# Short groups of a mixture of experts: output columns in fourths of TensorE's columns, and one scatter of short rows per group

## The chip, the core and the metric

The kernel runs on one core of a Trainium2 chip. The metric is the device time of one execution in microseconds (us), as the median of several runs. A profile of one execution gives every instruction's start and length on the core's engines: TensorE (PE, with its weight loads shown apart as PEld), VectorE (DVE), ScalarE (ACT), GpSimd (POOL) and SyncE (SP).

## What is computed

A block of a Perceiver: a cross attention from 8 x 64 tokens to 1601 context rows, a causal linear attention with an MLP, and a mixture of eight experts, all in fp32. The change lies in the mixture of experts:

```python
def _L0_ffn_ref(hidden_states, w_router, w0, w1, wo):
    ...
    x = hidden_states.reshape(-1, h)             # 512 tokens of 512 values
    router_logits = x @ w_router
    top_w, top_i = jax.lax.top_k(router_logits, K)          # K = 2 of 8 experts
    top_w = jax.nn.softmax(top_w.astype(jnp.float32), axis=-1).astype(x.dtype)
    gating = jnp.zeros((t, e), dtype=x.dtype).at[jnp.arange(t)[:, None], top_i].add(top_w)
    out = jnp.zeros_like(x)
    for ei in range(e):
        hmid = jax.nn.silu(x @ w0[ei]) * (x @ w1[ei])       # 1024 hidden values
        out = out + gating[:, ei:ei + 1] * (hmid @ wo[ei])
    return out.reshape(b, s, h)

...
x = x + _L0_ffn_ref(_layernorm(x, axis=-1), L0_ffn_w_router, L0_ffn_w0, L0_ffn_w1, L0_ffn_wo)
```

## The kernel before

All engines run the order in which the source writes their instructions (`tc.manual_schedule` names TensorE, VectorE, ScalarE, GpSimd and SyncE). The first 380 us are the two attentions, the MLP and the router; they are not touched, but for a few constants made at the start.

**The expert stage.** The router's result is turned into tables that list, for each expert, the tokens it has. Each expert takes its first 128 tokens as a whole tile (`whole_tile`, L1736). Its weights come by SyncE's queue into a ring of twelve 1 MB tiles: four `e_up` tiles, one for each fourth of the 1024 hidden values (`up_of`), and two `e_wo` tiles (`down_of`). A whole tile forms four up products (L1747; weights stationary, 128 tokens moving, 128 columns at a time), each followed by a SiLU on ScalarE and a product on VectorE (`gated`, L1703), and then eight products with `e_wo` (L1763) that gather in one PSUM bank. Of these eight, three are held back: `rest(0)`, `rest(1)` and `rest(2)` of the tile, which are passed on as `fill(k)` and put between steps that would leave TensorE waiting. The last of them is followed by `add_rows` (L1710): ScalarE multiplies by the gate, and GpSimd adds the rows to the output in HBM by an indirect DMA (L1726). GpSimd also fetches token rows by indirect DMA (`fetch`, L1663), for expert e + 2 while expert e runs. The scatters all write the output tensor, and each waits for the one before it.

**Tokens beyond 128.** They are taken by a branch at run time (`few_or_fill`, L2095, and `few_tokens`, L2085): none, one group of at most 32 tokens (`group`, L1800), or three groups of 32 (`three_groups`, L1844); there are copies of both bodies for every expert. With this input the experts have 133, 104, 217, 159, 87, 132, 70 and 122 tokens, so experts 0, 3 and 5 run `group` and expert 2 runs `three_groups`.

**A group.** With 32 tokens, the tokens are the stationary operand and take only 32 of TensorE's 128 columns. Four such products run beside each other, in four column fourths, each with its own moving operand; their results lie in four partition fourths of one PSUM bank. NQ is 4, R is 32, REST is 96.

- The up product (L1809 or L1864): column fourth q has the q-th fourth of the hidden values, 512 columns (both halves of the gated unit) moving.
- `gated`, and two transposes (`ht`, L1820 or L1876), whose result VectorE copies to SBUF (`hidT`, L1822 or L1878): hidden values on partitions, and for each fourth q its 32 tokens.
- The down product (`yq`, L1827 or L1884): column fourth q multiplies the hidden values of fourth q by the matching rows of `e_wo`, all 512 output columns moving. So the bank holds four partial sums, one in each partition fourth.
- Both halves of the bank are copied to SBUF (`parts`), and a product with `fold`, a 128 x 32 matrix of four stacked identities, adds the four partition fourths (L1841; in `three_groups` L1896, with all three groups in one bank).
- `add_rows` scales by the gate and scatters rows of 2 KB: 32 rows, or 96 for three groups.

In `group` the order on TensorE is: the transposes of the group's tokens and of the next expert's (`turn_next`), the up product, fill(0), the transposes of the hidden tile, fill(1), the down product, fill(2), the fold. In `three_groups` it is: up 0, up 1, turn 0, up 2, turn 1, down 0, turn 2, down 1, down 2, `turn_next`, the three fills, the folds.

PSUM has eight banks here: three of side 0, two of side 1 (`side_bank(1, ...)`, used in turn), and the single banks y0, y1 and yw (`y_bank`).

Of the kernel before, what the change touches and what calls it, by code (L numbers as in the profile page):

```python
# [15 lines left out]
F32 = mybir.dt.float32  # L16
# [4 lines left out]
P = 128  # L21
# [12 lines left out]
NQ = 4  # L34
# [9 lines left out]
NIDLE = 8  # L44
NS = 2
TWICE = 3
# [4 lines left out]
def perceiver_kernel(  # L51
# [186 lines left out]
    for i in range(NIDLE):  # L238
        n = 2 if i < TWICE else 1
        nc.tensor.matmul(  # L240
            idle_bank[:, : n * P],
            ident,
            ident[:, None, :].to_broadcast([P, n, P]),
            start=True,
            stop=True,
        )
# [1394 lines left out]
    if True:  # L1641


        def side_bank(side, name):
            return pse.tile([P, 512], F32, tag=f"mm{side}", bufs=3 - side, name=name)
# [153 lines left out]

        def group(e, up_of, down_of, fill, turn_next):  # L1800
# [21 lines left out]
            nc.vector.tensor_copy(h_t.rearrange("p j q -> p (j q)"), bank[:, : 2 * P])  # L1822
            fill(1)
            bank = side_bank(1, f"yq_{nm}")
            for j in range(2):
                for q in range(NQ):
                    nc.tensor.matmul(  # L1827
                        bank[q * R : (q + 1) * R, :],
                        h_t[:, j, q * R : (q + 1) * R],
                        down_of[q // 2][:, 2 * (q % 2) + j, :],  # L1830
                        start=(j == 0),
                        stop=(j == 1),
                    )
            parts = moe2.tile([P, D], F32, tag="parts3", bufs=3, name=f"parts_{nm}")
            halves = [slice(n * D // 2, (n + 1) * D // 2) for n in range(2)]
            nc.vector.tensor_copy(parts[:, halves[0]], bank[:, halves[0]])
            nc.scalar.copy(parts[:, halves[1]], bank[:, halves[1]])
            fill(2)
            y = y_bank(1, f"y_{nm}")
            for n in range(2):  # L1840
                nc.tensor.matmul(y[:R, halves[n]], fold, parts[:, halves[n]], start=True, stop=True)  # L1841
            add_rows((e, 1), [y], R, 1)

        def three_groups(e, up_of, down_of, fill, turn_next):  # L1844
# [12 lines left out]
            hid, h_t, sums, parts = {}, {}, {}, {}  # L1857
# [22 lines left out]
            def down(g):  # L1880
                bank = sums[g] = side_bank(1, f"yq_{nm}_{g}")
                for j in range(2):
                    for q in range(NQ):
                        nc.tensor.matmul(  # L1884
                            bank[q * R : (q + 1) * R, :],
                            h_t[g][:, j, q * R : (q + 1) * R],
                            down_of[q // 2][:, 2 * (q % 2) + j, :],
                            start=(j == 0),
                            stop=(j == 1),
                        )  # L1890
                parts[g] = moe2.tile([P, D], F32, tag="parts3", bufs=3, name=f"parts_{nm}_{g}")

            halves = [slice(n * D // 2, (n + 1) * D // 2) for n in range(2)]

            def folded(g, n):
                nc.tensor.matmul(  # L1896
                    y[g * R : (g + 1) * R, halves[n]], fold, parts[g][:, halves[n]], start=True, stop=True
                )
# [9 lines left out]
            down(1)  # L1908
            nc.vector.tensor_copy(parts[1], sums[1])
            down(2)  # L1910
            nc.vector.tensor_copy(parts[2][:, halves[0]], sums[2][:, halves[0]])
            nc.scalar.copy(parts[2][:, halves[1]], sums[2][:, halves[1]])
# [3 lines left out]

            y = y_bank(1, f"y3_{nm}")
            for g, n in [(0, 0), (1, 0), (2, 0), (0, 1), (1, 1), (2, 1)]:
                folded(g, n)
            add_rows((e, 1), [y], REST, 1)  # L1920

        if True:

            def late_places():
                nc.vector.tensor_tensor(late[:, 0, :, 0], late[:, 0, :, 0], late[:, 1, :, 0], ALU.add)
                src, dst = places(late[:, 0, :, 0], NE * NI, "late")
                for e in range(NE):
                    for i in range(2):
                        k = NI * e + i
                        slots[e, i] = (src[:, k : k + 1], dst[:, k : k + 1])  # L1930

# [188 lines left out]
            for e in range(NE):  # L2120
                turns = {}

                def between(k, e=e, turns=turns):
                    if k == 0 and e < NE - 1:
                        hint_ahead(e)
                    if e == 0 and k == 0:
                        late_places()
# [136 lines left out]
```

## Time and profile before

| | |
|---|---|
| median of 3 runs | 609.11 us (609.05 to 609.19) |
| profiled execution | 608.81 us |
| its span, first to last instruction | 607.1 us |
| mean granted TensorE clock | 0.996 |
| expert stage, from the first up product of expert 0 | 382.4 us on |
| expert 0's group, transposes to the next expert | 401.17 to 411.87 us |
| expert 2's three groups | 452.25 to 474.35 us |
| expert 3's group | 493.13 to 504.08 us |
| expert 5's group | 544.46 to 555.16 us |
| last scatter starts | 600.63 us |
| indirect scatters to the output | 11 of whole tiles and groups, 2 halves of the last tile |

Times within the profile count from the first instruction. PE busy is the time in which a matmul streams or drains; the matmuls are pipelined, so the recorded length of one (0.6 us for 512 columns) is more than the step to the next (0.43 us). "x16" in a line of the timeline is the number of passes merged into it; one fp32 product is two passes. The text in brackets says how long the engine had been idle and what ended that.

### The profile page before, as it was taken

The page shows a single profiled execution, that of the slowest core. Times are in us where ns is not written, and L with a number is a line of the kernel's source. Part 1 is how long each engine was busy: PE and PEld are TensorE (multiplying, and loading weights), DVE is VectorE, ACT ScalarE, POOL GpSimd, SP SyncE. Part 2 cuts the span into 40 slices and gives each one's busy share as a digit, 9 for nine tenths or more (in the row PEclk, how much of TensorE's full clock was granted, in tenths as well). Part 3 has the DMA queues.
Part 4 walks back from the last instruction along what each step waited for, and adds up shares of the span by engine and source line. Part 5 has one row for each costly group of instructions (what it writes and reads, how often), then busy time and mean ns, then how long its engine had stood idle before and what let it go on. Part 6 is the DMA issues. An engine that isn't in the chain of part 4 may idle for free.

```text
span 607.1 us, 9506 instructions
## 1 busy us (share of the span) xinstructions
PE 594.3 (98%) x3798; PEld 394.6 (65%) x3798; DVE 186.1 (31%) x450; ACT 152.7 (25%) x319; POOL 198.8 (33%) x266
## 2 busy tenths in 40 slices
PE   8999999999999999999999999999999999999994
PEld 6543434343477777668888758949772848775793
DVE  4121414234502667875104245411212111111100
ACT  3241314131136656333112311301001101001010
POOL 4000000000179987876996012342300121301112
PEclk9999999999999999999999999999999999999998
DMA  8999999999702003221236413259670959687411
GB/s 335 418 420 419 417 419 415 422 419 410 314 2 69 2 3 139 71 70 39 101 139 253 160 72 131 85 160 372 241 258 3 350 169 391 212 291 289 169 21 18
DMA packets 24087, 131.88 MB, mean 217 GB/s; under 512 B 4388, under 2 KB 4644, under 8 KB 12632
## 3 DMA queue, kind: packets, MB, share of 16 engines
q1 hardware_dynamic: 19496, 122.36, 50.9%
q0 software_dynamic: 3424, 7.61, 5.3%
q10 hardware_dynamic: 1104, 1.07, 0.5%
q8 instruction: 40, 0.66, 0.4%
q14 instruction: 23, 0.19, 0.1%
HBM read 126.08 MB, written 4.94 MB: 216 GB/s over the span
## 4 chain that ended last, share of the span: by engine, by line
PE 61%; DMA 23%; issue 13%; DVE 1%; ACT 1%; POOLq 1%; SPq 0%; POOL 0%; DVEq 0%
DMA out_dram<-y_sb,dst_late 15%; PE side L1163 8%; PE sc L481 7%; PE av L542 7%; DMA xg<-mn_dram,src_late 6%; PE v L627 5%; PE wk L788 4%; PE wq L788 4%; PE mlp L1249 3%; PE wo L999 3%; PE xo L576 2%; PE shared L1277 2%; PE up L1747 2%; DMA ctxT<-in_ctx_T_dram 2%; PE pw L407 2%
## 5 line engine op out<-in xcount | busy, mean ns | idle before, releaser
L1747 PEld LDWEIGHTS up<-xgT,e_up 128*128 128x128 f32 x896 | 100.7, 192 | 3.9 <-issue 2.1
L1747 PE MATMUL up<-xgT,e_up 128*128 128x128 f32 x896 | 101.6, 275 | 0.5 <-PEq L2149 0.3
L1726 POOL DMA_INDIRECT out_dram<-y_sb,dst_late x11 | 16.7, 1521 | 144.7 <-ACT y_sb L1717 108.0
L1763 PE MATMUL y<-e_wo,mid 128*128 128x512 f32 (+1 forms) x144 | 59.1, 549 | 0.0
L1707 DVE TENSOR_TENSOR mid<-up,act 128x256 f32<-128x256 f32 x38 | 16.1, 424 | 135.0 <-ACT act L1705 130.0
L590 POOL TENSOR_TENSOR h_sums<-h_t 128x256 f32<-128x256 f32 x1 | 0.7, 728 | 143.9 <-PE avt L569 143.9
L481 PE MATMUL sc<-ctxT,pw_t 128*64 128x401 f32 (+1 forms) x256 | 46.6, 503 | 0.3 <-DMA ctxT<-in_ctx_T_dram 0.3
L1705 ACT ACTIVATE act<-up 128x256 f32<-128x256 f32 x38 | 14.6, 383 | 119.5 <-PE up L1747 94.1
L542 PE MATMUL av<-ctx,eT 128*64 128x512 f32 x192 | 44.0, 595 | 0.0
L1763 PEld LDWEIGHTS y<-e_wo,mid 128*128 128x128 f32 x144 | 25.7, 190 | 23.0 <-issue 20.8
L481 PEld LDWEIGHTS sc<-ctxT,pw_t 128*64 128x64 f32 x256 | 17.7, 136 | 27.6 <-issue 26.2
L1163 PE MATMUL side<-v_sb,sum_w 128*128 128x256 f32 x128 | 30.5, 380 | 0.2 <-DVE v_sb L590 0.2
L542 PEld LDWEIGHTS av<-ctx,eT 128*64 128x64 f32 x192 | 13.7, 136 | 25.7 <-issue 24.8
L627 PE MATMUL v<-wv,h_t 128*128 128x512 f32 x64 | 29.2, 597 | 0.0
L922 DVE RECIPROCAL rden<-rden 128x512 f32<-128x512 f32 x8 | 26.8, 3344 | 1.4 <-ACT rden L915 1.4
L1163 PEld LDWEIGHTS side<-v_sb,sum_w 128*128 128x128 f32 x128 | 24.2, 190 | 3.9 <-issue 0.6
L1249 PE MATMUL mlp<-w,hid_sb 128*128 128x512 f32 (+1 forms) x50 | 22.3, 583 | 0.0
L489 ACT ACTIVATE scores<-sc,pb 128x401 f32<-128x401 f32 (+1 forms) x16 | 9.5, 591 | 46.6 <-PE sc L481 46.6
L498 DVE TENSOR_REDUCE negmax<-scores 128x1 f32<-128x1601 f32 x4 | 7.3, 1821 | 42.5 <-ACT scores L489 42.5
L627 PEld LDWEIGHTS v<-wv,h_t 128*128 128x128 f32 x64 | 11.6, 190 | 13.0 <-issue 12.5
L1666 POOL DMA_INDIRECT xg<-mn_dram,src_late x16 | 16.6, 1035 | 10.2 <-DVE dst_late L1660 5.7
L1186 ACT ACTIVATE hid_sb<-hid_sb,col 128x256 f32<-128x256 f32 (+1 forms) x16 | 9.8, 615 | 29.8 <-DVE hid_sb L1220 21.1
(372 smaller groups left out, 955.5 us busy)
## 6 DMA issues: line engine op xcount, KB each, us to landing
e_up<-in_L_ffn_up_dram SPq DMA_DIRECT2D x32, 1024.0 KB
ctx<-in_ctx_dram SPq DMA_DIRECT2D x24, 1024.0 KB
ctxT<-in_ctx_T_dram SPq DMA_DIRECT2D x24, 802.0 KB
e_wo<-in_L_ffn_wo_dram SPq DMA_DIRECT2D x16, 1024.0 KB
w<-in_L_attn_w_dram SPq DMA_DIRECT2D x8, 1024.0 KB
ctxT<-in_ctx_T_dram SPq DMA_DIRECT2D x8, 796.0 KB
wv<-in_L_attn_wv_dram SPq DMA_DIRECT2D x2, 1024.0 KB
wq<-in_L_attn_wq_dram SPq DMA_DIRECT2D x2, 1024.0 KB
```

The source lines that it names most:

```text
L481: nc.tensor.matmul(sc[h * S : (h + 1) * S, :width], pw_t[:, c, (2 * t + h) * S : (2 * t + h + 1) * S], keys[h][:, c, :], start=(c == 0), s ...
L542: nc.tensor.matmul(av[h * S : (h + 1) * S, :], e_t[:, 4 * g + j, h * S : (h + 1) * S], rows[h][:, j, :], start=(g == 0 and j == 0), stop=F ...
L627: nc.tensor.matmul(bank, h_t[:, c, t * P : (t + 1) * P], wv_n[:, c, :], start=(c == 0), stop=(c == KC - 1))
L788: nc.tensor.matmul(bank[:, :HT], weights[:, c, :], rows[:, c, :], start=(first and c == 0), stop=(c == 1), skip_group_check=True,)
L922: nc.vector.reciprocal(rden, rden)
L999: nc.tensor.matmul(wo_banks[t][:, part], row, weight, start=(start and j == js[0]), stop=(rows is None and j == nj - 1), skip_group_check= ...
L1163: nc.tensor.matmul(bank[:, :HT], weights[:, c, :], rows[:, c, :], start=(first and c == 0), stop=(c == 1), skip_group_check=True,)
L1249: nc.tensor.matmul(acc[t][:, part], hid[:, t * P : (t + 1) * P], w[:, part], start=False, stop=(f == FF // P - 1), skip_group_check=True,)
L1666: nc.gpsimd.indirect_dma_start(out=xg[:n, :], out_offset=None, in_=mn_dram, in_offset=bass.IndirectOffsetOnAxis(ap=slots[key][0][:n, :], a ...
L1726: nc.gpsimd.indirect_dma_start(out=rows, out_offset=bass.IndirectOffsetOnAxis(ap=where[:n, :], axis=0), in_=y_sb[:n, part], in_offset=None ...
L1747: nc.tensor.matmul(bank[:, m * P : (m + 1) * P], up_of[q][:, c, m * P : (m + 1) * P], xg_t[c], start=(c == 0), stop=(c == KC - 1),)
L1763: nc.tensor.matmul(bank[:, :width], h_t[:, j * P : (j + 1) * P], w[:, 2 * (q % 2) + j, n * width : (n + 1) * width], start=(q + j == 0), s ...
```

## The change

The kernel after the change splits the down product of a group the other way. Column fourth n holds output columns 128 n to 128 n + 127, and every one of the eight chunks of hidden values is multiplied in all four fourths: the same stationary tokens in each, 128 moving columns instead of 512. The bank's partition fourth n then holds the finished sums of 32 tokens for 128 output columns, and nothing has to be folded.

Gates and destinations must be spread to the four partition fourths as well. `spread_gates` does that for the gates, in each group or once for three groups, by a product with `fold`; `late_quarters` and `spread_places` do it once for all destinations, in expert 0's whole tile. The output is seen as rows of 128 values (four for each token), and each group is scattered by itself, as 128 rows of 512 bytes. In `group` VectorE scales the rows, in `three_groups` ScalarE, VectorE and ScalarE. New constants are made on GpSimd at the start, and the idle matmuls at the start are cut differently.

```diff
-NIDLE = 8
+NIDLE = 5
...
-TWICE = 3
+TWICE = 1
...
-        n = 2 if i < TWICE else 1
+        n = 3 if i < TWICE else 2
...
+    spread = const.tile([P, NQ, R], F32, name="spread")
+    for q in range(NQ):
+        nc.gpsimd.tensor_copy(spread[:, q, :], fold)
+    in_group = const.tile([P, NQ - 1], F32, name="in_group")
+    nc.gpsimd.memset(in_group, 0.0)
+    which_quarter = const.tile([P, 1], F32, name="which_quarter")
+    for q in range(NQ):
+        nc.gpsimd.memset(which_quarter[q * R : (q + 1) * R, :], float(q))
+        if q < NQ - 1:
+            nc.gpsimd.memset(in_group[q * R : (q + 1) * R, q : q + 1], 1.0)
...
+        out_quarters = out.rearrange("t (n d) -> (t n) d", n=NQ)
+        DQ = D // NQ
+
+        def in_quarters(bank, hid, moving, columns, start, stop):
+
+            for q in range(NQ):
+                nc.tensor.matmul(bank[q * R : (q + 1) * R, columns], hid(q), moving(q), start=start, stop=stop)
+
+        def spread_gates(e, groups, nm):
+
+            mine = moe2.tile([P, NQ - 1], F32, tag="gates_of", name=f"gates_of_{nm}")
+            nc.vector.tensor_scalar(mine[:REST, :], in_group[:REST, :], slots[e, 1][2][:REST, :], None, ALU.mult)
+            bank = side_bank(1, f"gates_{nm}")
+            in_quarters(
+                bank, lambda q: fold[:REST, :], lambda q: mine[:REST, :groups], slice(0, groups), True, True
+            )
+            gates = moe2.tile([P, NQ - 1], F32, tag="gates", name=f"gates_{nm}")
+            nc.vector.tensor_copy(gates[:, :groups], bank[:, :groups])
+            return gates
+
+        def down_chunks(y, g, h_t, j, down_of, first, last):
+
+            for q in range(NQ):
+                in_quarters(
+                    y,
+                    lambda n: h_t[:, q * R : (q + 1) * R],
+                    lambda n: down_of[q // 2][:, 2 * (q % 2) + j, n * DQ : (n + 1) * DQ],
+                    slice(g * DQ, (g + 1) * DQ),
+                    first and q == 0,
+                    last and q == NQ - 1,
+                )
+
+        def add_quarters(e, g, y, gates, by_vector):
+
+            y_sb = moe2.tile([P, DQ], F32, tag="ysq", bufs=3, name=f"y_sq_{e}_{g}")
+            rows, gate = y[:, :DQ], gates[:, g : g + 1]
+            if by_vector:
+                nc.vector.tensor_scalar(y_sb, rows, gate, None, ALU.mult)
+            else:
+                nc.scalar.activation(y_sb, rows, AF.Copy, scale=gate)
+            k = e * (NQ - 1) + g
+            nc.gpsimd.indirect_dma_start(
+                out=out_quarters,
+                out_offset=bass.IndirectOffsetOnAxis(ap=dst_quarters[:, k : k + 1], axis=0),
+                in_=y_sb,
...
+                compute_op=ALU.add,
+            )
+
         def group(e, up_of, down_of, fill, turn_next):
...
+            gates = spread_gates(e, 1, nm)
             fill(1)
-            bank = side_bank(1, f"yq_{nm}")
+            y = y_bank(1, f"yq_{nm}")
             for j in range(2):
-                for q in range(NQ):
-                    nc.tensor.matmul(
...
-            parts = moe2.tile([P, D], F32, tag="parts3", bufs=3, name=f"parts_{nm}")
...
+                down_chunks(y, 0, h_t[:, j, :], j, down_of, j == 0, j == 1)
             fill(2)
-            y = y_bank(1, f"y_{nm}")
-            for n in range(2):
-                nc.tensor.matmul(y[:R, halves[n]], fold, parts[:, halves[n]], start=True, stop=True)
-            add_rows((e, 1), [y], R, 1)
+            add_quarters(e, 0, y, gates, True)
...
             up(0)
             up(1)
             turn(0)
             up(2)
+            gates = spread_gates(e, NQ - 1, nm)
             turn(1)
-            down(0)
-            nc.scalar.copy(parts[0], sums[0])
-            turn(2)
...
+            for g in range(3):
+                ys[g] = (y_bank if g == 2 else side_bank)(1, f"yq_{nm}_{g}")
+                down(g)
+                add_quarters(e, g, ys[g], gates, g == 1)
+                if g == 0:
+                    turn(2)
             turn_next()
             for k in range(3):
                 fill(k)
-
-            y = y_bank(1, f"y3_{nm}")
-            for g, n in [(0, 0), (1, 0), (2, 0), (0, 1), (1, 1), (2, 1)]:
-                folded(g, n)
-            add_rows((e, 1), [y], REST, 1)
...
+            def late_quarters(dst):
...
+                nc.vector.tensor_copy(dst_f, dst.rearrange("p (e i) -> p e i", i=NI)[:, :, 1])
+                rows = moe.tile(by_group, F32, name="dst_groups")
+                nc.vector.tensor_tensor(
...
+            def spread_places(rows):
...
+                nc.tensor.matmul(
+                    bank[:, :n],
+                    spread.rearrange("p q r -> p (q r)"),
+                    rows.rearrange("p e g -> p (e g)"),
...
+                nc.vector.tensor_scalar(dst_quarters, bank[:, :n], float(NQ), which_quarter, ALU.mult, ALU.add)
...
                     if e == 0 and k == 1:
+                        spots_of["rows"] = late_quarters(spots_of["dst"])
                         few_of.extend(load_few())
+                    if e == 0 and k == 2:
+                        spread_places(spots_of["rows"])
```

More of the change, by code (lines that the diff above doesn't have):

```diff
@@ L1798, in whole_tile @@
             return rest
+        out_quarters = out.rearrange("t (n d) -> (t n) d", n=NQ)
[35 more added lines that the diff above has]
+                in_=y_sb,
+                in_offset=None,
+                bounds_check=NQ * (B * S + P) - 1,
+                oob_is_err=True,
+                compute_op=ALU.add,
+            )
         def group(e, up_of, down_of, fill, turn_next):
@@ L1822, in group @@
             nc.vector.tensor_copy(h_t.rearrange("p j q -> p (j q)"), bank[:, : 2 * P])
+            gates = spread_gates(e, 1, nm)
             fill(1)
-            bank = side_bank(1, f"yq_{nm}")
+            y = y_bank(1, f"yq_{nm}")
             for j in range(2):
-                for q in range(NQ):
[L1827 to L1833, printed above, removed]
-            parts = moe2.tile([P, D], F32, tag="parts3", bufs=3, name=f"parts_{nm}")
-            halves = [slice(n * D // 2, (n + 1) * D // 2) for n in range(2)]
-            nc.vector.tensor_copy(parts[:, halves[0]], bank[:, halves[0]])
-            nc.scalar.copy(parts[:, halves[1]], bank[:, halves[1]])
+                down_chunks(y, 0, h_t[:, j, :], j, down_of, j == 0, j == 1)
             fill(2)
-            y = y_bank(1, f"y_{nm}")
-            for n in range(2):
-                nc.tensor.matmul(y[:R, halves[n]], fold, parts[:, halves[n]], start=True, stop=True)
-            add_rows((e, 1), [y], R, 1)
+            add_quarters(e, 0, y, gates, True)
         def three_groups(e, up_of, down_of, fill, turn_next):
@@ L1855, in three_groups @@
             nc.vector.tensor_copy(xg_t3.rearrange("p c q -> p (c q)"), bank[:, : KC * REST])
-            hid, h_t, sums, parts = {}, {}, {}, {}
+            hid, h_t, ys = {}, {}, {}
             def up(g):
@@ L1880, in down @@
             def down(g):
-                bank = sums[g] = side_bank(1, f"yq_{nm}_{g}")
                 for j in range(2):
[L1883 to L1898, printed above, removed]
+                    down_chunks(ys[g], 0, h_t[g][:, j, :], j, down_of, j == 0, j == 1)
             up(0)
@@ L1903, in three_groups @@
             up(2)
+            gates = spread_gates(e, NQ - 1, nm)
             turn(1)
-            down(0)
-            nc.scalar.copy(parts[0], sums[0])
-            turn(2)
[L1908 to L1912, printed above, removed]
+            for g in range(3):
[4 more added lines that the diff above has]
+                    turn(2)
             turn_next()
@@ L1930, in late_places @@
                         slots[e, i] = (src[:, k : k + 1], dst[:, k : k + 1])
+                return dst
+            dst_quarters = moe.tile([P, NE * (NQ - 1)], mybir.dt.uint32, name="dst_quarters")
+            def late_quarters(dst):
+                by_group = [P, NE, NQ - 1]
+                dst_f = moe.tile([P, NE], F32, name="dst_f")
+                nc.vector.tensor_copy(dst_f, dst.rearrange("p (e i) -> p e i", i=NI)[:, :, 1])
+                rows = moe.tile(by_group, F32, name="dst_groups")
+                nc.vector.tensor_tensor(
+                    rows,
+                    dst_f[:, :, None].to_broadcast(by_group),
+                    in_group[:, None, :].to_broadcast(by_group),
+                    ALU.mult,
+                )
+                return rows
+            def spread_places(rows):
+                n = NE * (NQ - 1)
+                bank = side_bank(1, "dst_quarters")
+                nc.tensor.matmul(
+                    bank[:, :n],
+                    spread.rearrange("p q r -> p (q r)"),
+                    rows.rearrange("p e g -> p (e g)"),
+                    start=True,
+                    stop=True,
+                )
+                nc.vector.tensor_scalar(dst_quarters, bank[:, :n], float(NQ), which_quarter, ALU.mult, ALU.add)
+            spots_of = {}
             few = moe.tile([P, NE], F32, name="few")
@@ L2126, in between @@
                     if e == 0 and k == 0:
-                        late_places()
+                        spots_of["dst"] = late_places()
                         for key in [(0, 1), (1, 0), (0, 0), (1, 1), (2, 0), (2, 1)]:
```

## The prediction

> **What bounds the kernel now.** The page first, then the timeline of one expert with few tokens beyond its 128.
>
> ```profile
> span 607.1 us, 9506 instructions
> PE 594.3 (98%) x3798; PEld 394.6 (65%) x3798; DVE 186.1 (31%) x450; ACT 152.7 (25%) x319; POOL 198.8 (33%) x266
> ```
>
> TensorE (PE) is busy for 594.3 of 607.1 us, and its longest waits for others in the expert stage are 0.3 us each. So the time moves by what TensorE executes and by the new waits that its program order meets. The profiled execution took 608.81 us, 1.7 more than its span; the median of the runs is 609.11, 0.30 above it. My sum is a difference, put on the median. The short groups run four times: L1809 has 96 passes (32 for each of experts 0, 3 and 5, `group`), L1864 96 (expert 2, `three_groups`). One fp32 product is two passes in the trace.
>
> The timeline of expert 0's group (start, length, engine, line), lines of fast weight loads left out:
>
> ```profile
> 406.75 0.44 PE L1820 MATMUL ht<-ident,mid 128*128 128x128 f32 x2
> ...
> 407.02 1.02 PE L1763 MATMUL y<-e_wo,mid 128*128 128x512 f32 x2
> ...
> 407.22 0.42 DVE L1822 COPY hidT<-ht 128x256 f32<-128x256 f32 x1 [0.53 <-PE ht L1820]
> ...
> 407.98 1.92 PE L1827 MATMUL yq<-e_wo,hidT 128*32 128x512 f32 x16
> ...
> 409.83 1.13 PE L1763 MATMUL y<-e_wo,mid 128*128 128x512 f32 x2
> ...
> 410.89 1.05 PE L1841 MATMUL y<-parts,fold 128*32 128x256 f32 x4
> ...
> 411.87 14.56 PE L1747 MATMUL up<-xgT,e_up 128*128 128x128 f32 x128
> ```
>
> The reader should see that fill(1), the product at 407.02, hides the 0.42 us copy of the transposed tile, and that fill(2) at 409.83 hides the copies of the parts. The fold at 410.89 is the only part of the old ending that TensorE pays for. Expert 2:
>
> ```profile
> 464.03 0.44 PE L1876 MATMUL ht<-ident,mid 128*128 128x128 f32 x2
> ...
> 464.40 1.92 PE L1884 MATMUL yq<-e_wo,hidT 128*32 128x512 f32 x16
> 464.58 0.42 DVE L1707 TENSOR_TENSOR mid<-up,act 128x256 f32<-128x256 f32 x1 [3.18 <-ACT act L1705]
> ...
> 470.69 2.74 PE L1763 MATMUL y<-e_wo,mid 128*128 128x512 f32 x6
> ...
> 473.36 1.06 PE L1896 MATMUL y<-parts,fold 128*32 128x256 f32 x12
> ```
>
> Here turn(1) starts at 464.03, as soon as the third up product has streamed, while VectorE is still to form that group's hidden tile (to 465.00).
>
> **Removed: the fold.** In `group`, from fill(2) to the next expert's first product it is 411.87 - 409.83 = 2.04 us. Without the fold fill(2) takes 0.54 for its first pass (409.83 to 410.37, by the records) and 0.43 for its second (weight loads of L1763 follow each other every 0.43 us), so 0.97. Coming back from the 32-column shape costs a little more: from the first up product to the first y product it is 14.39 us after a group (411.87 to 426.26), 14.29 where none precedes (525.79 to 540.08). Gain 2.04 - 0.97 + 0.10 = **1.17 us**. In `three_groups` six passes of 0.43 from 470.69 end at 473.27, and the next expert starts at 474.35: gain 1.08 + 0.10 = **1.18**. The copies of the parts on VectorE and ScalarE go too; they lie beside fill(2) and are worth nothing.
>
> **Changed: the down product.** Before, 16 passes in 4 sets of four, 512 columns each, from 407.98 to 409.83: 4 x 0.43 + 0.13 to drain. After, 64 passes in 16 sets of 128 columns: as many streamed columns, four times the instructions. The trace has no 32-column product with 128 moving columns. From below: pure streaming, 0.43/4 = 0.107 a set, no change. From above: the weight load (109 ns, mean of L1827) not hidden at all, 0.217 a set, +1.75 a group. The nearest rows are the sets of four 64x64 products in the attention, here from the chain of waits:
>
> ```profile
> 198.94 0.46 PE nd L902 x32
> 199.40 0.47 PE qk L869 x32
> ```
>
> 32 passes, eight sets, in 0.47: 0.058 a set, where 64 columns stream in 0.054, though one load takes 135 ns. So loads hide, with some 5 ns a set over. The up product, 128 passes of 128 columns in 14.37 us, gives the same: 0.112. I take 0.112: 16 x 0.112 + 0.13 = 1.92, **+0.07 a group**; six groups, three of them in expert 2 (+0.22).
>
> The records of L902 show matmuls of one set starting 6 to 7 ns apart. [...]
>
> **Added: the gates, on the path.** `spread_gates` puts a VectorE product (`mine`), four one-column TensorE products and a copy ahead of fill(1). TensorE takes its program in order, so fill(1) stands behind the gates' product, which waits for `mine`, which stands behind the copy of the transposed tile on VectorE. Copy ends 407.22 + 0.42 = 407.64. A small VectorE operation takes about 0.16 (L1518 0.17) and may start 0.08 before its predecessor ends (423.65 against 423.31 + 0.42): `mine` runs 407.56 to 407.72. From VectorE's end to TensorE's start is 0.06 (406.27 + 0.42 to 406.75). The gates' product: the drain of 0.13 above plus 0.03 to 0.11 for its second pass, taken as 0.20. So fill(1) loads at 407.98 instead of 406.92: **+1.06 a group**. Fill(1) then hides nothing, since the copy is long done; the down product is what is late next, by the same 1.06. In expert 2 the gates stand between the third up product and turn(1), and `mine` behind the hidden tile that ends at 465.00: 465.08, + 0.06 + 0.20 = 465.34 against 464.03, **+1.31**. The bounds: 0.20 (the product alone, if nothing held it) and 1.5 (each VectorE step as dear as a copy from PSUM, 0.42, and each hop doubled).
>
> **Added once.** `spread_places` is two passes behind expert 0's y products: four passes of the router took 0.44 (378.30 to 378.74), so **+0.22**. Its input, two VectorE operations, is ready near 398.4, the product comes at 401.1; gone late it would cost its lateness. The idle matmuls at the start have the same 1,408 columns in 10 passes instead of 16; they end at 5.99, and the next product waits for VectorE until 6.87: 0, with 0.9 us of cover. GpSimd's twelve new setup steps (about 1.5 us by rows of 0.10 and 0.18) delay a memset that nobody waits for.
>
> **Moved: the scatters.** A group's rows go as 128 rows of 512 bytes, for 32 of 2 KB: the same bytes. Expert 2 has four scatters for two, and each waits for the landing of the one before:
>
> ```profile
> 474.43 1.59 POOL L1726 DMA_INDIRECT out_dram<-y_sb,dst_late  x1 [35.38 <-ACT y_sb L1717]
> 485.60 1.46 POOL L1726 DMA_INDIRECT out_dram<-y_sb,dst_late  x1 [9.58 <-DMA out_dram<-y_sb,dst_late]
> 487.36 1.09 POOL L1666 DMA_INDIRECT xg<-mn_dram,src_late  x1 [0.30 <-issue]
> ```
>
> Behind them on GpSimd's queue are the fetches of expert 5, at 487.36 now. At worst four scatters of 11 us from 468.3 hold them until 512; landed after 4 us (the median) they are there at 516, and TensorE turns that tile at 522.77. The cover is 6 us; a fetch as slow as the slowest (11.4) would cost under 1 us. No later wait on the output tiles follows, since these have two and three buffers, and GpSimd is idle before the last scatters (16.50 us). SP's weight loads are released by TensorE and shift with it. I take 0.
>
> **The sum.** Groups: 3 x (1.06 + 0.07 - 1.17) = -0.1. Expert 2: 1.31 + 0.22 - 1.18 = +0.35. Expert 0: +0.22. Together **+0.45 us: 609.6 us**. The change removes four folds and pays for them with four waits.
>
> **The rivals.** *A, faster: the gates cost no wait.* If the gates' product finds its input ready, each place pays 0.20 instead of 1.06 or 1.31: groups 3 x -0.90, expert 2 -0.76, expert 0 +0.22, together -3.2: **605.9**. For it speaks that `mine` needs nothing of the group; against it, the trace has all engines in written order. *B, slower: code.* The short groups' code is longer, and jumps pass over it. TensorE's branches, from the views of the two lines (count, then least, median and greatest ns):
>
> ```profile
> L2096 PEldq COMPARE_BRANCH  x6: 77/92/4305, 396.1 to 539.2; - x6
> L2090 PEldq COMPARE_BRANCH  x8: 80/248/4747, 396.2 to 554.2; - x8
> ```
>
> Two took 4.3 and 4.7 us, and work queued ahead hid them: the 4.7 us from 539.4 ended 0.3 before the transposes at 544.46. At the end of expert 2's group the branch comes 3.06 us ahead of the next product (471.29 to 474.35) and took 0.19; as slow as the two, it would cost 4.3 to 4.7 less 3.1, about 1.4, and one more such jump nearly hidden 0.3: +0.45 + 1.7, **611.3**. It decides from the point where a jump lasts longer than the queued work. [...] *C, much slower: loads not hidden.* 6 x 1.75 less the 0.44 counted: +10.5, **619.6**; the 64x64 rows speak against it.
>
> **How the numbers follow.** Forecast 0.48, A 0.21, B 0.23, C 0.08. A measurement here can tell about 0.2% (1.2 us) from no change, so the forecast, whose own range is 608.5 to 610.4, falls within it; A is faster; B and C, with some mishaps of the forecast, are slower: 0.21, 0.48, 0.31. The range reaches half into A and beyond B: 606.0 to 612.3.
>
> **What would show it.** Fill(1) some 1.0 us later after the transposes, led by a wait for VectorE's `mine`; a down product of 1.9 us; no fold, with the next up product 0.97 after fill(2); four scatters in expert 2. Fill(1) straight after the transposes speaks for A, a TensorE gap at a branch for B, sets of 0.2 us for C. I am wrong if TensorE's order isn't the written one, or a set of four isn't 0.112.

## The result and the profile after

| | before | after |
|---|---|---|
| median | 609.08 us (608.87 to 609.24, 6 runs) | 613.74 us (612.62 to 615.48, 6 runs) |
| profiled execution | 608.81 us | 613.95 us |
| mean granted clock of the runs | 0.996 in the profiled one | 0.991 to 0.996 |

The changed kernel is slower by 0.8%, clear of the spread of the runs: ratio 1.0077, interval 1.0067 to 1.0087. The page of the changed kernel:

```profile
span 612.2 us, 10138 instructions
PE 593.4 (97%) x4090; PEld 403.4 (66%) x4090; DVE 187.3 (31%) x460; ACT 148.8 (24%) x312; POOL 204.2 (33%) x280
```

TensorE is busy for 0.9 us less than before, and the span is 5.1 us longer: it stands idle for longer (and a stretch at half clock, shown below, counts as busy). The timeline of expert 0's group:

```profile
407.55 0.44 PE L1881 MATMUL ht<-ident,mid 128*128 128x128 f32 x2
408.02 0.42 DVE L1883 COPY hidT<-ht 128x256 f32<-128x256 f32 x1 [0.53 <-PE ht L1881]
408.36 0.22 DVE L1821 TENSOR_SCALAR gates_of<-in_group,xg 96x3 f32<-96x3 f32 x1
...
408.73 0.24 PE L1816 MATMUL gates<-gates_of,fold 96*32 96x1 f32 x8 [0.74 <-DVE gates_of L1821]
...
408.90 1.12 PE L1773 MATMUL y<-e_wo,mid 128*128 128x512 f32 x2
...
409.96 1.96 PE L1816 MATMUL yq<-e_wo,hidT 128*32 128x128 f32 x64
...
411.84 1.12 PE L1773 MATMUL y<-e_wo,mid 128*128 128x512 f32 x2
...
412.80 0.38 PE L1757 MATMUL up<-xgT,e_up 128*128 128x128 f32 x2
```

It shows what was forecast: fill(1) waits for `mine` (named `gates_of`), the down product takes 1.88 us (409.96 to 411.84) and no fold follows. The next expert's product, the last line, starts 0.96 us after fill(2). The end of expert 2's three groups, and TensorE's waits in the expert stage (line waited at, releaser: us, times, longest):

```profile
466.30 0.44 PE L1924 MATMUL ht<-ident,mid 128*128 128x128 f32 x2
...
472.55 0.66 PE L1705 MATMUL xgt<-ident,xg 128*128 128x128 f32 x4
...
473.04 2.74 PE L1773 MATMUL y<-e_wo,mid 128*128 128x512 f32 x6
...
478.03 2.29 PE L1757 MATMUL up<-xgT,e_up 128*128 128x128 f32 x10 [2.25 <-issue]
```

```profile
PE gates L1816 <- DVE gates_of L1821: 3.4, 4, 1.2
PE up L1757 <- issue: 2.3, 1, 2.3
```

Between the fills and expert 3's first product TensorE stands for 2.25 us with nothing to wait for that the profile shows. The view of the branch line, with its greatest value, says what its sequencer did (count, least, median and greatest ns):

```profile
L2148 PEldq COMPARE_BRANCH  x8: 80/376/5842, 399.1 to 558.7; - x8
```

The 5.84 us belong to the jump at the end of expert 2's three groups, over its one-group body and the path without few tokens. It begins at 472.02 and ends at 477.86. Before, it took 0.19 us, as the view of the same line there shows for 470.5 to 473 us:

```profile
L2090 PEldq COMPARE_BRANCH  x1: 192/192/192, 471.2 to 471.2; - x1
```

Then the granted clock, in windows over the same place (length, busy PE, clock, DMA share, GB/s):

```profile
478.00:478.50 0.50, 0.47 (x3) 0.73 1.01 426
478.50:481.50 3.00, 3.00 (x16) 0.50 1.02 426
481.50:482.00 0.50, 0.50 (x6) 0.85 0.96 396
```

After the gap TensorE runs at half clock, for 3.4 us by these windows. The same work, set beside the trace of before, is later by:

| place | later by, us | step |
|---|---|---|
| first transposes; 94 us on | 1.04; 0.65 | the start |
| behind `spread_places` | 0.80 | +0.15 |
| expert 1's first y product | 0.83 | expert 0's group, +0.03 |
| expert 2, `turn_next` | 2.35 | +1.52 |
| expert 3's first up product | 3.68 | no fold, -1.08; the jump, +2.41 |
| expert 3's first y product | 5.28 | half clock, +1.60 |
| after experts 3 and 5 | 5.14 | their groups, -0.14 |

So 4.66 of the 5.14 us come from three things that the sum doesn't hold: the start, the jump and the clock.

### The profile page after: what moved, and what is told of

The parts are those of the page before. It is cut to its first block, busy times and chain, and to the rows that moved or that the text cites. A ratio compares the mean times of both kernels' runs of the same rounds, so it can differ in the third digit from the quotient of the medians.

```text
span 612.2 us, 10138 instructions
## 1 busy us (share of the span) xinstructions
PE 593.4 (97%) x4090; PEld 403.4 (66%) x4090; DVE 187.3 (31%) x460; ACT 148.8 (24%) x312; POOL 204.2 (33%) x280
## 5 line engine op out<-in xcount | busy, mean ns | idle before, releaser
L1757 PEld LDWEIGHTS up<-xgT,e_up 128*128 128x128 f32 x896 | 102.6, 194 | 6.6 <-issue 6.6
L1757 PE MATMUL up<-xgT,e_up 128*128 128x128 f32 x896 | 103.0, 278 | 2.6 <-issue 2.3
L1736 POOL DMA_INDIRECT out_dram<-y_sb,dst_late x7 | 11.1, 1591 | 73.4 <-ACT y_sb L1727 62.3
L1851 POOL DMA_INDIRECT out_dram<-y_sq,dst_quarters x6 | 9.4, 1562 | 71.3 <-ACT y_sq L1849 29.5
```

The costliest lines, as they stand in the source:

```text
L1736: nc.gpsimd.indirect_dma_start(out=rows, out_offset=bass.IndirectOffsetOnAxis(ap=where[:n, :], axis=0), in_=y_sb[:n, part], in_offset=None ...
L1757: nc.tensor.matmul(bank[:, m * P : (m + 1) * P], up_of[q][:, c, m * P : (m + 1) * P], xg_t[c], start=(c == 0), stop=(c == KC - 1),)
```

## Experiments

Each is the changed kernel or the kernel before with one edit; intervals are of the ratio to runs of before on the same chip (medians 608.78 to 608.99).

**Is the jump what stalls?** First without its length, `x_short`:

```diff
                 with three.Else():
+                    if e == 2:
+                        turn_next()
+                        return
                     group(e, up_of, down_of, fill, turn_next)
```

> The changed kernel with the one-group body of expert 2 left out; this input never runs it, but TensorE's jump at the end of expert 2's three groups passes over it. Jump theory (that jump, 5.84 us for 0.19 before, is most of the loss: 2.3 us of idle TensorE, then 1.6 us more while its clock is granted at half): the jump takes about 0.2 us, no idle before expert 3's first up product, clock 1.00 there, 609.8 us. Waits theory (the four waits for the gates cost more than the folds gave, the jump is only where it shows): 613.7 us, the idle time moved elsewhere. Start theory (the start, 0.65 us later, and nothing else of one place): 613.7.

Measured 611.14 us, 1.0034 (1.0023 to 1.0044). The jump took 0.20 us and TensorE didn't wait: some 2.5 us of the loss are back (2.15 us above the kernel before on that chip, for 4.66). The timeline shows expert 3 following its fills without a bracket:

```profile
474.11 2.74 PE L1773 MATMUL y<-e_wo,mid 128*128 128x512 f32 x6
476.69 9.54 PE L1757 MATMUL up<-xgT,e_up 128*128 128x128 f32 x84
```

The time stays above the 609.8 expected: this run's start is 1.13 us late, and the last two down products took 4.11 us for 3.70, with a gap of 0.27 us in the weight loads that nothing but issue explains (`x_small` below has the same, 4.10 us). Then the kernel before with a longer body to jump over, `b_long`:

```diff
-            for j in range(2):
+            for j in [*range(2), *(26 * [0, 1] if e == 2 else [])]:
                 nc.tensor.transpose(bank[:, j * P : (j + 1) * P], hid[:, j * P : (j + 1) * P], ident)
```

> The kernel before, with 52 more transposes (104 instructions) in the one-group body of expert 2, which this input never runs; nothing that is executed changes, and the jump at the end of expert 2's three groups passes over some 264 instructions as in the changed kernel, for 160. Jump theory: the jump takes 4.3 to 5.9 us, TensorE idles 1.3 to 2.8 us before expert 3 and runs at half clock after it, 611.5 to 613.5 us. Waits theory and start theory: 609.1 us.

Measured 610.09 us, 1.0014 (1.0005 to 1.0024). The branch view of its line:

```profile
L2090 PEldq COMPARE_BRANCH  x8: 80/316/4102, 396.6 to 555.8; - x8
```

The 4.10 us are this jump, from 471.57 to 475.67; the next product starts at 475.84 after 1.06 us of idle time. Code that never runs made the old kernel slower by the mechanism of rival B, with a smaller stall than expected and no half clock; so the median lies below the 611.5 to 613.5 of the jump theory.

**Does queued work cover it?** `x_hold` leaves the jump and puts more work ahead of it. The held products stand in each of expert 2's paths, so they also lengthen the code that is passed over:

```diff
-            for q in range(NQ - 1 if len(y) == 1 else 0):
-                down(q, hid[q], range(2) if q < NQ - 2 else [0])
+            held = 7 if key == (2, 0) else 3
+            chunks = [(q, j) for q in range(NQ) for j in range(2)]
+            for q, j in chunks[: 2 * NQ - held] if len(y) == 1 else []:
+                down(q, hid[q], [j])
...
+                for q, j in chunks[2 * NQ - held : -2] if k == 0 else [chunks[k - 3]]:
+                    down(q, hid[q], [j])
```

> The changed kernel, with seven instead of three of the eight y products of expert 2's whole tile held back as fills, so that they stand at the end of its three groups, behind the same code. The same work, in another order. Theory (the jump over the one-group body is long, and costs only what the queued work does not cover): the jump still takes 3.5 to 7 us, but 14 passes of 0.43 us are queued ahead of it, so no idle time and no half clock before expert 3's first product: 610 to 611 us, and expert 3 some 2.7 us behind the kernel before instead of 5.3. Rival (what is lost there is not the jump's cover but transfers or a clock that this stage loses anyway): 613 to 614 us with an idle time of 2 us in the same place.

Measured 610.68 us, 1.0031 (1.0019 to 1.0042). The branch view and the timeline:

```profile
L2148 PEldq COMPARE_BRANCH  x8: 80/340/6582, 400.0 to 556.9; - x8
```

```profile
470.65 6.17 PE L1773 MATMUL y<-e_wo,mid 128*128 128x512 f32 x14
476.94 9.28 PE L1757 MATMUL up<-xgT,e_up 128*128 128x128 f32 x81
```

The jump took 6.58 us, from 470.18 to 476.76; 14 passes stood in front of it, TensorE lost about 0.3 us (the last of them and expert 3's first product start 0.70 us apart, 0.43 in `x_short`), and the clock stayed at 1.00. As a control, `b_hold` holds the same products back in the kernel before.

> The kernel before, with seven of expert 2's eight y products held back to the end of its three groups, as in the changed kernel of the run before. It tells whether the held products are worth anything without the change. Theory (they only cover a long jump, and the kernel before has none there): 608.7 to 609.3 us. Rival (they are a gain, or a loss, of their own): 607 to 608, or 610 and more.

Measured 608.91 us, 0.9999 (0.9990 to 1.0007): held products are worth nothing where no jump is long.

**What does the stall cost without a jump?** `b_stall` makes TensorE wait for VectorE in the same place:

```diff
-                copy(xg_t.rearrange("p c q -> p (c q)"), bank[:, : KC * n])
+                for _ in range(9 if key == (3, 0) else 1):
+                    copy(xg_t.rearrange("p c q -> p (c q)"), bank[:, : KC * n])
```

> The kernel before, in which VectorE copies expert 3's transposed tile nine times instead of once, so that TensorE waits for VectorE at expert 3's first up product, with no code changed around the jump. It measures what a wait of some 2 to 3 us in this place costs by itself. Theory (such a wait is followed in part of the executions by some 3.4 us at half clock): an idle time of 2 to 3 us, runs that lie between 2 and 4.5 us above the kernel before and spread over 1.5 us or more: a median of 611.5 to 613. Rival (the half clock belongs to the late jump, not to the wait): the wait alone, 611 to 612, runs within 0.5 us of each other, and a granted clock of 1.00 behind it.

Measured 612.85 us, 1.0063 (1.0048 to 1.0079). The windows of its profile (length, busy PE, PEld, DVE, ACT and POOL, clock, DMA share, GB/s):

```profile
474.00:478.00 4.00, 0.94 (x11) 0.55 (x6) 3.24 (x5) 0.83 (x2) 1.60 (x1) 1.00 0.96 338
478.00:482.00 4.00, 4.00 (x24) 4.00 (x23) 0.00 (x0) 0.00 (x0) 0.00 (x0) 0.59 1.05 364
```

A wait of 3.1 us (expert 3 starts 3.13 later than before) became 4.72 by its first y product, again 1.6 for half clock. The runs fall apart: 611.93, 612.03 and 612.14 with a mean clock of 0.996 to 0.997, which is the wait alone; 613.57 and 613.65 with 0.994; 614.63 with 0.992. The clock loss followed a wait of 2.25 us behind the jump of the change and one of 3.06 us behind VectorE's copies here, in some executions. That accounts for much of the spread of the changed kernel's runs.

**Is it the distance or the place?** `x_idle` cuts the idle matmuls as before, which puts all later code 12 instructions further on (`NIDLE = 8`, `TWICE = 3`, `n = 2 if i < TWICE else 1`); `b_idle` is the reverse, the kernel before with the new cut.

> The changed kernel with the idle matmuls of the start cut as before: 16 passes for 10, so all later code of TensorE lies 12 instructions further on. Theory (the start does not depend on the idle matmuls; the jump at expert 2's end is long because of the code it passes over, wherever that lies): first transposes at 7.5 to 7.9 us, a jump of 3.5 to 7 us, 612 to 615 us. Rival (the jump is long because of where the code lies): a jump of 0.2 us and 609.5 to 611.

> The kernel before with the idle matmuls of the changed one (10 passes, of 384 and 256 columns, for 16). Start theory (the idle matmuls make the first transposes 1.0 us later, of which 0.65 stays): 609.8 us. Otherwise 609.1 us, with the first transposes at 6.9 us. As the code lies 12 instructions earlier, the jump theory leaves room for a changed branch.

Measured for `x_idle` 614.36 us (1.0079, 1.0059 to 1.0099) and for `b_idle` 609.53 (1.0007, 0.9998 to 1.0017). The cut doesn't touch the start: `b_idle`'s transposes start at 6.82 us, 6.87 before. `x_idle`'s jump took 6.31 us; and in `b_idle` expert 5's jump, over code that is the same, took 6.41 us for 4.75 and cost 1.43 us. That profile is of `b_idle`'s slowest run, of 608.81 to 610.27, so this price is not that of every run. `x_small` leaves out the bodies that this input doesn't run, but not expert 2's:

```diff
                 with tc.If(few_of[e] == 1, label=f"three_{e}") as three:
-                    three_groups(e, up_of, down_of, fill, turn_next)
+                    if e == 2:
+                        three_groups(e, up_of, down_of, fill, turn_next)
+                    else:
+                        turn_next()
+                        for k in range(3):
+                            fill(k)
                 with three.Else():
-                    group(e, up_of, down_of, fill, turn_next)
+                    if e in (0, 2, 3, 5):
+                        group(e, up_of, down_of, fill, turn_next)
+                    else:
+                        turn_next()
+                        for k in range(3):
+                            fill(k)
```

> The changed kernel without the bodies of code that this input does not run: three groups for all experts but 2, one group for experts 1, 4, 6 and 7; expert 2 keeps both of its bodies. What is computed for this input is the same. Theory of the start (x lands later because the whole program is longer): x's first tile lands at 4.5 to 4.9 us and the first transposes start near 6.9, as in the kernel before, and the end jump of expert 2, over the same code, is still 3.5 to 7 us: 612 to 613.5. Rival (the start depends on something else in the change): x lands at 5.1 to 5.9 us, 612.6 to 615.5 as the changed kernel.

Measured **609.58 us** (609.34 to 609.87, 11 runs), 1.0011 (1.0002 to 1.0020). The first tile of x landed at 4.47 us, as the theory of the start has it; but neither side had expected that expert 2's jump over the same code took 2.17 us and was hidden.

```profile
L2148 PEldq COMPARE_BRANCH  x8: 80/212/2171, 398.0 to 554.0; - x8
```

So the distance isn't the whole cause. `x_cut67` leaves out only the bodies of experts 6 and 7 (in both arms `if e < 6:`), so that the program is shorter and no code in front moves; `b_more` adds 1536 never-run transposes there to the kernel before (in `three_groups`, `192 * [*range(KC)] if e >= 6`).

> The changed kernel without the never-run bodies of experts 6 and 7, the last in the program: all code of experts 0 to 5, run or not, stands where it stood. What is computed for this input is the same. Theory (length): expert 2's end jump shorter than 3.6 us, so hidden, x's first tile at 4.4 to 5.1 us, 609.5 to 611 us. Rival (the jump's length comes from the code just around it): a jump of 5 to 7 us, 612.5 to 615 us.

> The kernel before with 1536 never-run transposes on TensorE, half in expert 6's three groups and half in expert 7's, behind everything that this input runs but the branch near the end that passes over them. Nothing in front of them moves, so only the program's length differs, by about what the change adds. Theory (the length by itself makes the start late and instruction loads slow): x's first tile lands at 5.1 to 6.1 us, 609.5 to 610.3 us, and the branches of experts 1 and 5 take as long as in the kernel before or longer. Rival (length alone does nothing; what the bodies left out in the run before last had done, they did by their place between the bodies that run): x at 4.4 to 4.9 us and 608.8 to 609.2.

Measured for `x_cut67` 612.47 us, 1.0073 (1.0057 to 1.0090): the start is nearly back (x at 4.86 us, 0.23 late at 94 us), the jump took 5.88 us. For `b_more` 609.82 us, 1.0014 (1.0005 to 1.0023): x at 5.12 us, TensorE 0.82 us late at 217 us and 1.10 at 545. A longer program by itself made the kernel slower, and in this trace its start later; the long jump it does not explain. How late the start comes, length alone does not say: `x_pad192` below is longer than the change, and its x landed at 4.87 us. Last, the place alone: `x_pad64`, `x_pad128` and `x_pad192` lengthen expert 0's never-run body.

```diff
-            for c in range(KC):
+            for c in [*range(KC), *(8 * [*range(KC)] if e == 0 else [])]:
                 nc.tensor.transpose(
```

(16 and 24 in the other two. 64, 128 and 192 are the instructions that this adds.)

> The changed kernel with 32 never-run transposes more in expert 0's three groups, so that everything of TensorE behind them lies 64 instructions further on, and what expert 2's end jump passes over is the same. Theory (where the jump and its target lie within the blocks in which instructions are loaded decides how many loads it waits for): of this run and the two with 128 and 192, at least one has an end jump of 0.2 to 2.5 us, no idle time behind it, and 609.5 to 611.5 us, and another has one of 5 to 7. Rival (the distance decides): all three jumps take 5 to 7 us, and 612 to 615.5.

> As the run with 64, with 64 never-run transposes: 128 instructions further on. Theory of place: see there. Rival of distance: a jump of 5 to 7 us, 612 to 615.5.

> As the run with 64, with 96 never-run transposes: 192 instructions further on. Theory of place: see there. Rival of distance: a jump of 5 to 7 us, 612 to 615.5.

| code in front moved by | expert 2's end jump | idle behind it | median, us | ratio |
|---|---|---|---|---|
| 0 (the change) | 5.84 us | 2.25 us | 613.74 | 1.0077 |
| 12 instructions | 6.31 | 2.73 | 614.36 | 1.0079 (1.0059 to 1.0099) |
| 64 | 2.61 | none | 610.46 | 1.0028 (1.0017 to 1.0039) |
| 128 | 1.51 | none | 611.68 | 1.0046 (1.0026 to 1.0065) |
| 192 | 0.60 | none, 1.79 later | 611.67 | 1.0048 (1.0028 to 1.0067) |

The jumps of the last three rows, each alone in its window:

```profile
L2148 PEldq COMPARE_BRANCH  x1: 2612/2612/2612, 471.8 to 471.8; - x1
L2148 PEldq COMPARE_BRANCH  x1: 1508/1508/1508, 472.2 to 472.2; - x1
L2148 PEldq COMPARE_BRANCH  x1: 595/595/595, 471.7 to 471.7; - x1
```

The rival of distance is out: none of the three took 5 to 7 us. The theory of place held in its main point and not in all: it asked for a jump of 5 to 7 us among the three and had none, and the two jumps under 2.5 us came with medians 0.2 us above its 611.5. So the place decides how long the jump is. Each length is of one execution, but code at the same place gave nearly the same in others: 5.84 and 5.88 us (`x_cut67`), and 0.19 to 0.20 in the kernel before, `b_const`, `b_stall` and `b_more`; and the slowest run of the three, 611.99 us, is faster than the fastest of the change, 612.62. A short jump here doesn't end the loss, as stalls come up elsewhere: with 128 TensorE waits 0.82 us at expert 4, at 526.26. With 192 the stream of instructions runs dry 13 passes behind the jump:

```profile
475.27 1.61 PE L1757 MATMUL up<-xgT,e_up 128*128 128x128 f32 x13
478.67 7.52 PE L1757 MATMUL up<-xgT,e_up 128*128 128x128 f32 x65 [1.79 <-issue]
```

The DMA queues of the changed kernel (packets, MB, share of the engines) show one that carries instructions, 16 KB a packet (the view of before has the same row, with 40 packets):

```profile
q8 instruction: 44, 0.72, 0.5%
```

The traces have the time of each packet, and with it what a jump waits for (us):

| | expert 2's end jump | packet of this queue | from its end to the jump's |
|---|---|---|---|
| before | 471.24 to 471.43 | 469.39 to 470.76 | 0.67 |
| the change | 472.02 to 477.86 | 475.50 to 476.42 | 1.44 |
| `x_idle` | 473.06 to 479.37 | 477.02 to 477.96 | 1.41 |
| `b_long` | 471.57 to 475.67 | 473.24 to 474.30 | 1.38 |
| `x_pad64` | 471.78 to 474.39 | 471.49 to 472.99 | 1.40 |
| `x_pad128` | 472.25 to 473.75 | 471.42 to 472.34 | 1.41 |
| `x_pad192` | 471.68 to 472.27 | 469.52 to 470.88 | 1.39 |

Each of the 74 jumps of TensorE over 0.5 us behind 380 us, in all 19 traces, ends 1.30 to 1.53 us after such a packet, and the gap of 1.79 us with 192 ends 1.41 after one. So a long jump here is one whose packet comes late: in the change it starts 3.48 us after the jump has begun, in the three runs with 64 to 192 it starts before the jump does. What makes it start late isn't shown.

**The gates early.** `x_early` puts VectorE's product first in each body and TensorE's ahead of the up product:

```diff
+            mine = gates_of(e, nm)
             turn_tile((e, 1), R)()
             turn_next()
+            gates = spread_gates(mine, 1, nm)
...
-            gates = spread_gates(e, 1, nm)
             fill(1)
```

> The changed kernel with the gates' VectorE product first in each body and their TensorE product ahead of the up products, where VectorE is long done. All theories agree on the waits themselves: four waits (1.2 us each) go, fill(1) covers the copy of the transposed tile again, 3 x 1.1 + 1.4 = 4.7 us less, 609.0 us with the jump as it is, 605.1 if the jump should be hidden by chance. If fold and gates had balanced only by chance of the trace: less than 3 us gained.

Measured 611.59 us, 1.0036 (1.0024 to 1.0047), for 609.0 expected. Each group became shorter than before the change (expert 0's by 0.72 us, expert 3's by 1.24, expert 5's by 1.05). Expert 2 gave 0.88 back, since its first up product's bank waited for the copy of the gates, behind that of the 96 transposed tokens; its jump took 7.04 us, and TensorE stood for 3.41. `x_best` mends both: the gates go into free columns of the bank of the 96 tokens, and seven products are held as in `x_hold`.

```diff
-            bank = side_bank(1, f"gates_{nm}")
+            columns = slice(at, at + groups)
+            if bank is None:
+                bank = side_bank(1, f"gates_{nm}")
...
+            gates = spread_gates(mine, NQ - 1, nm, bank, KC * REST)
```

> The same with the gates taken early: VectorE's product of the gates first of all in each body, TensorE's four small products ahead of the up product; for three groups into the free columns of the bank of the 96 transposed tokens, so that no up product waits for their copy. Theory (each group has a wait of 0.9 us for VectorE ahead of fill(1), which the early product avoids, and expert 2 has 1.2 us of the same): 610.5 less 3 x 0.9 less 1.0, so 606.5 to 607.5 us, faster than the kernel before. Rival (code, whose position has changed again, makes other jumps late): 608 to 611 with an idle time behind a branch at expert 1, 2, 4 or 5.

Measured **607.12 us** (606.17 to 607.88, 8 runs), 0.9967 (0.9956 to 0.9978): faster than both kernels. Fill(1) now follows the transposes of expert 3's group at once, as before the change:

```profile
499.45 0.44 PE L1887 MATMUL ht<-ident,mid 128*128 128x128 f32 x2
499.73 1.02 PE L1773 MATMUL y<-e_wo,mid 128*128 128x512 f32 x2
500.68 1.96 PE L1816 MATMUL yq<-e_wo,hidT 128*32 128x128 f32 x64
```

The 5.34 us jump is covered; elsewhere, in expert 1's up products, TensorE has a gap of 0.84 us that nothing but issue explains:

```profile
415.04 12.33 PE L1757 MATMUL up<-xgT,e_up 128*128 128x128 f32 x109 [0.84 <-issue]
```

`x_best_idle` moves that code by 12 instructions, with the old idle cut.

> The version with early gates and held products, with the idle matmuls of the start cut as in the kernel before, so that all later code of TensorE lies 12 instructions further on and nothing else differs. It measures what the place of the code is worth by itself. Theory (stalls of the instruction stream of 0.3 to 1 us move from place to place): 606 to 608.5, with the gap of 0.84 us in expert 1's up products gone or moved. Rival (the gap belongs to the work there): the same 607.1 within 0.3 us and a gap in the same place.

Measured 607.55 us, 0.9983 (0.9966 to 0.9999). The gap in expert 1 is gone, the start is 1.30 us late for 1.03, and one of seven runs took 610.84. The medians of the two, taken on different chips, lie 0.43 us apart and their intervals overlap, so the gap did move with the code, but what the move is worth can't be told.

**The constants.** `b_const` has the three new constants in the kernel before, unused.

> The kernel before with the three new constants made at the start and not used. Theory of the start (the constants shift the placing in SBUF or delay the first transfers): x's first tile lands 0.4 to 0.7 us later and the first transposes start at 7.5 to 7.9 instead of 6.9 us: 609.6 to 610.1. Rival (the later start belongs to the longer program, whatever it holds): start as in the kernel before, 608.9 to 609.3.

Measured 609.00 us, 1.0001 (0.9991 to 1.0010), x at 4.90 us: they are not the late start.

## Why the prediction was wrong

What it said of the work held; what it said of code did not.

- **Removed: the fold**, 1.17 a group: from fill(2) to the next product it is 0.96 us (411.84 to 412.80) for 2.04, and 0.10 came back in the next up products: 1.18. Right.
- **Changed: the down product**, +0.07: 1.88 for 1.85 us. Right: 64 passes in 1.88 us are one in 29 ns, and the records of one set start 6 to 7 ns apart, as in L902 before. In expert 2 the last 32 sets took 3.70 us with the drain, for 3.71 by the same reckoning.
- **Added: the gates, on the path**, +1.06: from the transposes to fill(1) it is 1.35 us for 0.27, so +1.08. In expert 2 turn(1) came 1.43 later for 1.31. `mine` took 0.22 for the 0.16 taken. Right, and rival A wrong as the kernel was written: it needed the order changed.
- **Added once**: `spread_places` 0.15 for 0.22, right. The idle matmuls cost nothing, right; but the start came 0.65 us later all the same.
- **Moved: the scatters**, 0: no wait of TensorE for fetched tokens shows after. Right.
- **The sum**, +0.45: with the never-run bodies gone, the same work took 609.58, 0.67 above the kernel before on that chip, for 609.6 forecast. That agreement is in part a balance (in its trace the start is 0.35 us earlier than before and expert 2's last products take 0.4 us more), but the steps of the change's own trace say the same: 5.14 less 4.66 leaves 0.48 for the work, for 0.45.

The step that failed is **the sum**: it took TensorE's instruction stream as unchanged. Expert 2's jump was left at 0.19 us, and the start at its old time. Rival B named the jump, its place and the point from which it decides, and was given 0.23; what it mis-sized was the price. B reckoned 4.3 to 4.7 less a lead of 3.1, about 1.4 us. The jump took 5.84 us and cost 2.41 (a lead of 3.4), and the stall brought half clock, 1.60 more, of which B had nothing. The late start, 0.65, stood in no case: of the start the prediction weighed the idle matmuls and GpSimd's setup, and not the length of the program. The three are 4.66 us; so the time lay beyond B and outside the range, though its mechanism was listed. B took the 4.3 and 4.7 us, two samples, as the most that a jump can last; and a branch that had taken 0.19 us in one trace, at one place of the code, was taken as one that stays short.

That the change put the jump into a bad place, rather than that any longer body would, is shown by the shifts of 64 to 192 instructions, and that the jump waited for a packet of instructions by the packets' times. Why that packet started only 3.48 us after the jump began isn't shown, nor how the longer program delays the first transfers. That half clock followed in the profiled execution was chance, by where the gap fell (see the last section): of `b_stall`'s six runs three show only the wait.

## What to carry to other kernels

Where an engine is busy 98% of the time, as here, never-run code counts (1.10 us in `b_long`, 1.04 in `b_more`): list each jump's duration, the instruction packet that it waits for and the work queued in front of it, and price a longer body as a stall with a chance (in these traces from none to 3.41 us), with the clock loss behind it (1.60 us in the trace of the change). A change of a few tenths of a per cent should be timed at several code positions, by padding a body that doesn't run, before it is kept or dropped. A small product that an engine in order must wait for goes to the top of the block, where its input is long ready: here that turned four waits of 1.1 to 1.4 us into a gain, together with the held products that cover the jump.

## What the hardware showed unexpectedly

- A jump over the same code took 0.60, 1.51, 2.61, 5.84 or 6.31 us as the code in front was moved by 192, 128, 64, 0 or 12 instructions; each ended 1.4 us after a 16 KB packet of instructions.
- 1536 never-run transposes at the program's end made the kernel 1.04 us slower. In that trace the first tile of x landed at 5.12 us, for 4.80 in the trace of before and 4.42 to 4.90 in those of its other variants.
- Half clock for 3.4 us came after idle times of 2.25 (the change), 2.73 (`x_idle`) and 3.06 us (`b_stall`), and in the profile not after 3.41 us (`x_early`) or 2.26 us (`x_cut67`). So the length of the gap alone does not decide it. The granted clock shows where the gaps fall. In these traces it changes on a grid of 3.41 us: in the change at 478.24, at 481.65 and again at 607.94, 38 such steps after the first; in `x_early` at 8.67 and 12.09 and then at 602.59. The windows of that grid about the gap, for the change, `x_idle`, `b_stall`, and two of `x_early` (length, busy PE, clock, DMA share, GB/s):

```profile
474.82:478.24 3.42, 1.17 (x5) 1.00 1.02 417
477.16:480.57 3.41, 1.03 (x9) 1.00 1.01 423
475.29:478.70 3.41, 1.22 (x11) 1.00 0.95 377
472.89:476.30 3.41, 1.87 (x5) 1.00 1.00 416
476.30:479.71 3.41, 1.54 (x14) 1.00 1.06 386
```

  Half clock came behind the first three, in which TensorE was idle for 2.2 to 2.4 us. The 3.41 us of `x_early` are cut by the grid into 1.54 and 1.87, and of `x_cut67`'s gap 1.79 lie in one window. So, as far as these traces go, the idle time within one window decides: in the expert stage 2.2 us were enough and 1.9 were not. At the kernel's start 1.9 us were enough (`x_early`, `x_hold`), so the limit isn't one number of idle time.
